# Attention score products in a two-layer kernel: row-mode steps planned as single products, sorted over the four row groups of TensorE

## The chip, the cores and the metric

The kernel runs on one core of a Trainium2 chip. The metric is the device time of one execution in microseconds (us). The kernel before takes 3334.01 us, the median of three runs (3331.4 to 3335.59). About 0.2% of this, some 7 us, is what a measurement of this kernel can tell from no change.

Engines are named as in the profile: PE is TensorE (PEld its weight loads), DVE is VectorE, ACT is ScalarE, POOL is GpSimd, SP is the queue that issues most DMAs.

## What is computed

The input x is (2, 2048, 256) in fp32. Each of two layers is `x = x + attn(norm(x)) * silu(ffn(norm(x)))`. The part that matters here is one causal softmax attention in each layer, with 16 heads of width 16 (first layer, inside its ffn) or 32 (second layer, where the real and the imaginary part of 16 each are one dot product of 32):

```python
scores = einsum('bhqd,bhkd->bhqk', q, k) / 4
scores = where(causal, scores, -1e9)          # -inf in the second layer
probs  = softmax(scores, axis=-1)
out    = einsum('bhqk,bhkd->bqhd', probs, v)
```

Around it the first layer has a linear attention, layer norms and a mixture of 8 experts (top 2, capacity 1024); the second has a quantized linear layer with a low-rank addition. All matrix products of scores and values are fp32.

## The kernel before

**Stages.** The first layer's attentions and routing run to about 1400 us, the experts to about 1917 us, the second layer's attention to the end.

**Heads and row groups.** Four heads form a group; a batch of 2 and 16 heads make 8 groups. A head's queries and keys lie in 32 partitions, so its score product needs 32 rows of the array, and the four heads of a group go to the four row groups 0 to 3 of PE, which work side by side ("row mode"; the profile shows such products as `32*128`). Sums of weighted values use four column groups ("col mode", `128*32`), and everything else the whole array ("all", `128*128`).

**Two passes over the scores.** Pass A (`pass_a`) computes scores of 128 queries by up to 512 keys, for the maximum of each query: L575 is the product (fp32, up to 512 columns), L594 the maximum on DVE over two heads at once. On the diagonal, the first layer adds the causal mask by four small bf16 products (`hide`, L534, 128, 96, 64 and 32 columns); the second layer masks on DVE instead (L588). Pass B (`pass_b`) computes the scores again, turned (keys by 256 queries): two products of up to 256 columns (L609), on the diagonal four bf16 mask products (`hide_pair`, L541, 256 down to 64 columns), in the second layer one or two bf16 products that subtract the maximum (`less_maximum`, L1697 to L1700), and then the exponential on ACT (L621). Sums over keys follow in col mode (L911, L1740, L1751); in the second layer POOL adds up the exponentials (L1717 to L1722).

**PSUM.** There are eight banks. A pair of heads of pass A takes two banks, one head of pass B takes one, and so does every other product. A bank comes free when DVE or ACT has read it.

**The order.** `run_attention` walks over units. A unit has one pass-A tile for the four heads of a group and, a little behind, one pass-B tile for four heads. Nothing is issued there: every piece of work becomes a step of a `Plan` (`S(strand, engine, cost, fn, reads, writes, on)`). Steps of one strand and engine stay in the order they were given. All row-mode and value-sum steps of PE form the strand "S"; other strands of PE (prep, lin, sub, end, mix, gate, ...) may go between them. `Plan.run` searches for an order: `advance` takes at each point the step that a model of the engines can start first (with offsets by strand), and a beam search varies the offsets. The steps are then issued in that order, engine by engine. So the order of all engines follows from the steps, their costs and the model.

**A unit's PE steps before.** For the heads i = 0, 1 of pass A and 2, 3 of pass B, and then the other way round: product A of head i, both products B of head i+2 as one step, product A of head i+1, both products B of head i+3 as one step; then the mask products, each head's four as one step (cost `T_HIDE_A` 0.15, `T_HIDE_B` 0.28).

**The model of PE before** (`advance`). A row group is taken until the cost of its last step has passed (`groups`); a step is handed out when its inputs are there and PE's queue is free, 0.01 us after the last; a load of 0.105 us is charged when a group was idle or the mode has just changed (`cold`).

Of the kernel before, what the change touches and what calls it, by code (L numbers as in the profile page):

```python
# [17 lines left out]
P = 128  # L18
# [76 lines left out]
class State:  # L95


    def __init__(self, plan):
# [9 lines left out]
        self.free, self.groups, self.cold = {}, [0.0] * 4, [True] * 4  # L108
# [12 lines left out]
class Plan:  # L121
# [101 lines left out]
    def advance(self, st, handicaps, until):  # L223

        free, groups, can, ready = st.free, st.groups, st.can, st.ready
        while st.todo:
# [4 lines left out]
            for key, s in can.items():  # L231
# [6 lines left out]
                if eng == "PE":  # L238
                    closed = strand != "S" and not (gap and st.used + s.cost <= self.LIMIT)
                    x = top if s.kind != st.mode else groups[s.on] if s.row else top - self.MODE  # L240
                    if x > busy:
                        busy = x
# [43 lines left out]
            if s.eng == "PE":  # L286
                st.used = st.used + s.cost if key[0] != "S" else 0.0
                kind = s.kind
                if kind != st.mode:
                    if kind == "row":  # L290
                        groups[:] = [max(t, x) for x in groups]
                    st.cold[:] = [True] * 4
                if s.row:
                    if t > groups[s.on] or st.cold[s.on]:
                        t += s.load
                    st.cold[s.on] = False
                elif t > max(groups) or st.cold[0]:
                    t += s.load
                    st.cold[0] = False
                done, free["PE"] = t + s.cost + self.TAIL - self.GAP, sent + 0.01  # L300
                if kind == "row":
                    st.mode, groups[s.on] = "row", t + s.cost
                    worth /= 4
                else:
                    st.mode, groups[:] = s.on, [t + s.cost] * 4
# [72 lines left out]
def kernel(ctx: ExitStack, tc: tile.TileContext, i: dict, out: bass.AP):  # L378
# [148 lines left out]
    T_HIDE_A, T_HIDE_B = 0.15, 0.28  # L527

    def hide(out, j, mask):

        r = slice(32 * j, 32 * j + 32)
        for q in range(4):
            cols = slice(32 * q, P)
            nc.tensor.matmul(out[:, cols], ident_h[r, q], mask[r, q, cols], start=False, stop=q == 3)  # L534

    def hide_pair(out, j, mask):

        r, v = slice(32 * j, 32 * j + 32), out.rearrange("p (n k) -> p n k", n=2)
        for q in (3, 2, 1, 0):
            cols = slice(0, 32 * q + 32)  # L540
            nc.tensor.matmul(v[:, :, cols], ident_h[r, q], mask[r, q, :, cols], start=False, stop=q == 0)  # L541
# [8 lines left out]
    def run_attention(plan, make, prepare, subtract, sum_keys, finish, last_sum, before=None, others=(), between=False, causal=None):  # L550
# [17 lines left out]
        def pass_a(g, t, k, i, w, mx, parts):  # L568
# [11 lines left out]
            def products(x):  # L580
                return S("S", "PE", t_row(w), lambda: score(x), r=[(g.qt, t), *((g.kt, n) for n in keys)], w=[(s, x)], on=i + x)

            def rest():
                for x in range(2) if diagonal and causal is None else ():
                    S("S", "PE", T_HIDE_A, lambda x=x: hide(s.t[:, x, w - P : w], i + x, mask_q), r=[(s, x), "ident_h", "mask_q"], w=[(s, x)], on=i + x)
# [15 lines left out]
        def pass_b(g, c, p, j, pt):  # L601
# [5 lines left out]
            def score():  # L607
                for n, (kj, q0, at) in enumerate(halves_of(c, p)):
                    nc.tensor.matmul(  # L609
                        s.t[:, at], g.kt.t[r, kj * P : (kj + 1) * P], g.qt.t[r, QC * c + q0 : QC * (c + 1)],  # L610
                        start=n == 0 and not ahead, stop=n == 1 and not (diagonal or before and not ahead),
                    )

            def rest():
                if before and not ahead:
                    S("S", "PE", 0.25 * t_row(w), before(g, c, j, s, diagonal, False, not diagonal), r=[s, g.mh[c]], w=[s], on=j, load=0.026)
                if diagonal:
                    S("S", "PE", T_HIDE_B, lambda: hide_pair(s.t[:, : 2 * P], j, mask_h), r=[s, "mask_h"], w=[s], on=j)
# [4 lines left out]
            reads = [(g.kt, 2 * p), (g.kt, 2 * p + 1), (g.qt, 2 * c), (g.qt, 2 * c + 1)]  # L623
            opener = None
            if ahead:
# [1256 lines left out]
```

## Time and profile before

| what | value |
|---|---|
| median of 3 runs | 3334.01 us |
| the profiled execution | 3333.86 us |
| its span, first to last instruction | 3332.1 us |
| mean granted TensorE clock | 0.982 |
| time up to the experts / the experts / second layer's attention | 0 to 1400 / 1400 to 1917 / 1917 to 3327 us |
| score products A (L575), records and busy time | 5120, 1282.3 us |
| score products B (L609), records and busy time | 9216, 1239.8 us |
| value sums (L911 and L1740) | 4608 records each, 269 us each |
| DVE maximum of two heads (L594), 1024 columns | 1221 ns |
| ACT exponential (L621), 512 columns | 602 ns |

How to read it: an fp32 product appears as two records, since it goes over the array twice (two "passes"); a bf16 product appears as one. A record of a matmul lasts from its start to the modelled end of its results, so the records of one group overlap, and the union "busy" says little about lost time. What tells the speed of a group is the distance between the starts of its records. In the timeline view, neighbouring records of one line are merged; a row gives start, length, engine, line, operation, tiles and shape, and a number of records.

### The profile page before, as it was taken

Reading aid. Unit: us, or ns where it says so; the run is one execution under the profiler, and the core shown is the slowest. Engines: PE = TensorE matmul, PEld = TensorE weight load, DVE = VectorE, ACT = ScalarE, POOL = GpSimd, SP = SyncE. Lnnn points to the kernel's source line nnn. Section 1 sums busy time; section 2 is a strip of 40 time slices with the busy share of each in tenths; the row PEclk is TensorE's granted clock in tenths of the full one; section 3 lists DMA queues with packets and bytes.
Section 4 is the critical chain, followed back from the end, with each engine's and each line's share of the span. In section 5 each row is a group of like instructions: output and inputs, shape, how many; then the busy total and the mean of one; then the engine's idle time right before and its main releaser. Section 6 shows DMA issues by size and latency. Waiting matters only on the chain.

```text
span 3332.1 us, 92022 instructions
## 1 busy us (share of the span) xinstructions
PE 3205.3 (96%) x39748; PEld 2271.7 (68%) x39748; DVE 2132.9 (64%) x4250; ACT 1623.4 (49%) x3264; POOL 1620.8 (49%) x2006
## 2 busy tenths in 40 slices
PE   7999999989999999979999989999999999999998
PEld 5677777767777776656666646666766666767775
DVE  5677677667777767641112057787777776777785
ACT  3565555555555555511112155555554555544554
POOL 5442222333233222310000057898987776878887
PEclk9999999999999999989999989999999999999999
DMA  5000000000000010133342131110101001000000
GB/s 198 2 2 2 5 8 8 17 30 26 6 11 5 9 45 13 49 109 115 109 131 94 64 105 43 38 43 29 39 17 33 27 17 40 23 12 23 14 29 24
DMA packets 99742, 134.51 MB, mean 40 GB/s; under 512 B 9461, under 2 KB 76739, under 8 KB 99334
## 3 DMA queue, kind: packets, MB, share of 16 engines
q1 hardware_dynamic: 93190, 114.74, 10.6%
q0 software_dynamic: 6144, 13.88, 1.3%
q8 instruction: 311, 5.10, 0.6%
q14 instruction: 97, 0.79, 0.1%
HBM read 93.75 MB, written 37.75 MB: 39 GB/s over the span
## 4 chain that ended last, share of the span: by engine, by line
PE 50%; DVE 3%; POOL 2%; ACT 1%; issue 1%; DMA 0%; POOLq 0%; another core or an unknown queue 0%; SPq 0%; DVEq 0%; ACTq 0%
PE banks L575 9%; PE banks L609 8%; PE banks L414 8%; PE banks L1740 7%; PE s L1488 7%; PE s L1494 7%; PE banks L1751 2%; PE banks L1700 1%; PE banks L541 1%; PE banks L1698 1%; DVE mx L594 1%; POOL ps L1721 1%; ACT pt L621 1%; POOL ps L1717 0%; POOL ps L1722 0%
## 5 line engine op out<-in xcount | busy, mean ns | idle before, releaser
L621 ACT ACTIVATE pt<-banks 128x512 f32<-128x512 f32 (+1 forms) x2304 | 1160.7, 577 | 721.9 <-PE banks L609 321.3
L594 DVE TENSOR_REDUCE mx<-banks 128x2 f32<-128x1024 f32 (+3 forms) x1024 | 1119.1, 1122 | 337.4 <-PE banks L609 141.7
L575 PE MATMUL banks<-carried,carried 32*128 32x512 f32 (+3 forms) x5120 | 1282.3, 566 | 25.0 <-DVE mx L594 10.5
L609 PE MATMUL banks<-carried,carried 32*128 32x256 f32 (+1 forms) x9216 | 1239.8, 378 | 3.8 <-issue 3.7
L609 PEld LDWEIGHTS banks<-carried,carried 32*128 32x128 f32 x9216 | 972.1, 186 | 42.8 <-issue 15.8
L575 PEld LDWEIGHTS banks<-carried,carried 32*128 32x128 f32 x5120 | 545.3, 185 | 242.3 <-issue 108.6
L1717 POOL TENSOR_TENSOR ps<-pt 128x1024 f32<-128x1024 f32 (+1 forms) x159 | 346.7, 2181 | 113.8 <-ACT pt L621 101.8
L1721 POOL TENSOR_TENSOR ps<-ps,pt 128x1024 f32<-128x1024 f32 x127 | 302.4, 2381 | 69.3 <-ACT pt L621 64.8
L848 POOL TENSOR_TENSOR ra<-raw,rope 128x128 f32<-128x128 f32 x128 | 60.1, 470 | 566.3 <-ACT raw L860 496.1
L1700 PE MATMUL banks<-mh,ones_h 3*128 3x512 bf16 x896 | 272.0, 382 | 7.5 <-ACT mh L1688 3.5
L1722 POOL TENSOR_TENSOR ps<-ps,pt 128x1024 f32<-128x1024 f32 (+1 forms) x127 | 269.1, 2119 | 10.0
L911 PE MATMUL banks<-pt,vt 128*32 128x256 f32 (+1 forms) x4608 | 269.1, 371 | 4.3 <-DVE mx L594 3.0
L1740 PE MATMUL banks<-pt,vt 128*32 128x256 f32 (+1 forms) x4608 | 269.0, 371 | 2.5 <-ACT pt L621 2.5
L1497 DVE TENSOR_TENSOR ye<-s,b 128x256 f32<-128x256 f32 x64 | 27.2, 424 | 380.6 <-PE s L1494 380.6
L588 DVE CUSTOM_DVE_ANT_0 banks<-banks,causal 128x384 f32<-128x384 f32 (+3 forms) x512 | 240.3, 515 | 40.5 <-PE banks L575 25.2
L1489 ACT ACTIVATE hm<-s,b1c 128x512 f32<-128x512 f32 x128 | 87.8, 687 | 347.2 <-PE s L1488 346.0
L1488 PE MATMUL s<-xt,carried 128*128 128x512 f32 x512 | 228.2, 604 | 9.7 <-DVE xt L1421 9.7
L1494 PE MATMUL s<-carried,hm 128*128 128x256 f32 x1024 | 223.6, 379 | 0.0
L1740 PEld LDWEIGHTS banks<-pt,vt 128*32 128x32 f32 x4608 | 135.2, 110 | 129.5 <-ACT pt L621 26.4
L1494 PEld LDWEIGHTS s<-carried,hm 128*128 128x128 f32 x1024 | 194.6, 190 | 33.3 <-issue 7.7
L911 PEld LDWEIGHTS banks<-pt,vt 128*32 128x32 f32 x4608 | 134.0, 109 | 114.4 <-issue 15.7
L1488 PEld LDWEIGHTS s<-xt,carried 128*128 128x128 f32 x512 | 97.4, 193 | 131.2 <-issue 110.2
(276 smaller groups left out, 4166.9 us busy)
## 6 DMA issues: line engine op xcount, KB each, us to landing
carried<-in_L_ffn_W_dram SPq DMA_DIRECT2D x32, 1024.0 KB
gl<-g_dram SPq DMA_DIRECT2D x64, 256.0 KB
slots_in<-zero SPq DMA_DIRECT2D x8, 1024.0 KB
slots_out<-ye SPq DMA_DIRECT2D x16, 512.0 KB
xe<-slots_in SPq DMA_DIRECT2D x15, 512.0 KB
s_dram<-lo SPq DMA_DIRECT2D x16, 256.0 KB
hn<-in_L_attn_x_dram SPq DMA_DIRECT2D x16, 256.0 KB
g_dram<-gs SPq DMA_DIRECT2D x16, 256.0 KB
```

Of the source, the lines that this page charges most:

```text
L575: nc.tensor.matmul(s.t[:, x, :w], g.qt.t[r, t * P : (t + 1) * P], g.kt.t[r, 512 * k : 512 * k + w], start=True, stop=not (diagonal and cau ...
L594: S("A", "DVE", t_dve(2 * w), lambda: nc.vector.tensor_reduce(mx.t[:, t % 2, i : i + 2, k], s.t[:, :, :w], AX.X, ALU.max), r=[(s, 0), (s, ...
L609: nc.tensor.matmul(s.t[:, at], g.kt.t[r, kj * P : (kj + 1) * P], g.qt.t[r, QC * c + q0 : QC * (c + 1)], start=n == 0 and not ahead, stop=n ...
L621: S("B", "ACT", t_act(w), lambda: nc.scalar.activation(pt.t[:, j, :w], s.t[:, :w], AF.Exp, scale=0.25), r=[s], w=[(pt, j)])
L911: nc.tensor.matmul(av.t[32 * j : 32 * j + 32, q0:QC], vts[G.vn][:, kj, j], pt.t[:, j, at], start=n == 0, stop=n == len(tiles) - 1,)
L1488: nc.tensor.matmul(ps, w1[:, k, f * P : (f + 1) * P], xt[:, k], start=k == 0, stop=k == 1)
L1494: nc.tensor.matmul(ps[:, :D], hm[:, f, s * P : (s + 1) * P], w2[:, f], start=f == 0, stop=f == FF // P - 1)
L1700: nc.tensor.matmul(s.t.rearrange("p (n q) -> p n q", n=2), ones_h[r], m[:, None].to_broadcast([3, 2, QC]), start=first, stop=last,)
L1717: nc.gpsimd.tensor_tensor(ps.t[:, :, q0:], pt.t[:, :, same], pt.t[:, :, odd], ALU.add)
L1721: nc.gpsimd.tensor_tensor(ps.t, ps.t, pt.t[:, :, even], ALU.add)
L1722: nc.gpsimd.tensor_tensor(ps.t[:, :, q0:], ps.t[:, :, q0:], pt.t[:, :, odd], ALU.add)
L1740: nc.tensor.matmul(av.t[32 * j : 32 * j + 32, q0:QC], G.vt.t[:, kj, j], pt.t[:, j, at], start=n == 0, stop=False)
```

## The change

1. `pass_a` and `pass_b` give their PE work as lists of single products: each mask product, each of the two products B, and each of the subtracting products is an entry of its own with its cost. The mask products of a head go in rising width instead of falling.
2. `run_attention` collects the entries of a whole unit in four queues, one for each row group (groups 0 and 1: A first, then B; groups 2 and 3: B first, then A). The summed costs of what is ahead give each entry the time at which the entry before it in its queue begins; entries are sorted by that time over all groups and become steps in this order. DVE and ACT steps follow after all PE steps of the unit. Steps of the paced strands (prep, lin, mix, gate) now wait for the unit's last PE step instead of its last product A.
3. The model: a row step cannot be handed out before the last step handed to its group has begun (`began`), so that a third step for one group holds PE's queue; a change of mode waits until all groups have ended, plus 0.1 us; the load is always counted from the time of handing out; a step takes 0.007 us of the queue instead of 0.01.

The arithmetic is the same. The core of the diff:

```diff
                 if eng == "PE":
+                    if s.row and s.kind == st.mode and began[s.on] > t:
+                        t = busy = began[s.on]
                     closed = strand != "S" and not (gap and st.used + s.cost <= self.LIMIT)
...
-                if kind != st.mode:
-                    if kind == "row":
-                        groups[:] = [max(t, x) for x in groups]
-                    st.cold[:] = [True] * 4
+                if s.kind != st.mode:
+                    sent = max(sent, max(groups) + self.MODE)
+                    st.mode, groups[:], began[:] = s.kind, [sent] * 4, [sent] * 4
                 if s.row:
-                    if t > groups[s.on] or st.cold[s.on]:
-                        t += s.load
-                    st.cold[s.on] = False
+                    t = max(groups[s.on], sent + s.load)
+                    began[s.on], groups[s.on] = t, t + s.cost
...
-                done, free["PE"] = t + s.cost + self.TAIL - self.GAP, sent + 0.01
+                done, free["PE"] = t + s.cost + self.TAIL - self.GAP, sent + 0.007
...
     def hide(out, j, mask):
-        for q in range(4):
-            cols = slice(32 * q, P)
-            nc.tensor.matmul(out[:, cols], ident_h[r, q], mask[r, q, cols], start=False, stop=q == 3)
+        for q in (3, 2, 1, 0):
+            cols = slice(32 * q, P)
+            parts.append((max(0.027, (P - 32 * q) / 2400), lambda q=q, cols=cols: nc.tensor.matmul(
+                out()[:, cols], ident_h[r, q], mask[r, q, cols], start=False, stop=q == 0
+            )))
...
             for i in (0, 2):
-                for x in range(2):
-                    if a:
-                        plan.pace = products(x)
-                        first = first or plan.pace
-                    if b:
-                        step, rest, weigh = pass_b(gb, cb, p, (i + 2 + x) % 4, pt)
-                        first = first or step
-                        more.append((rest, weigh))
-                if a:
-                    after_a()
-                for rest, _ in more:
-                    rest()
-                for _, weigh in more:
-                    weigh()
+                    for x in range(2):
+                        queues[i + x] += products(x)
+                    after.append(after_a)
+                for j in ((i + 2) % 4, (i + 3) % 4) if b else ():
+                    products, weigh = pass_b(gb, cb, p, j, pt)
+                    queues[j] += products()
+                    after.append(weigh)
+            order = []
+            for j, q in enumerate(queues):
+                began, until = -1.0, 0.0
+                for n, entry in enumerate(q):
+                    order.append((began, j, n, entry))
+                    began, until = until, until + entry[0]
+            order.sort(key=lambda x: x[:3])
+            for _, j, _, (cost, fn, r, w_, load) in order:
+                step = S("S", "PE", cost, fn, r=r, w=w_, on=j, load=load)
+                first = first or step
+            if a:
+                plan.pace = step
+            for call in after:
+                call()
```

## The prediction

> **What bounds the kernel now.** First the page: PE is busy nearly all the time in both attention stages, and the chain that ended last runs over PE where it can be followed.
>
> ```profile
> span 3332.1 us, 92022 instructions
> PE 3205.3 (96%) x39748; PEld 2271.7 (68%) x39748; DVE 2132.9 (64%) x4250; ACT 1623.4 (49%) x3264; POOL 1620.8 (49%) x2006
> ...
> PE 50%; DVE 3%; POOL 2%; ACT 1%; issue 1%; DMA 0%; POOLq 0%; another core or an unknown queue 0%; SPq 0%; DVEq 0%; ACTq 0%
> ```
>
> Then the windows of the three stages (length, busy time of PE, PEld, DVE, ACT, POOL):
>
> ```profile
> 10.00:1400.00 1390.00, 1350.05 (x17078) 998.39 (x17078) 986.48 (x1865) 779.37 (x1661) 448.05 (x1071) 0.99 0.07 23
> 1400.00:1917.00 517.00, 488.04 (x1840) 325.04 (x1839) 93.22 (x265) 106.59 (x160) 31.29 (x49) 0.97 0.32 105
> 1917.00:3327.00 1410.00, 1366.38 (x20833) 947.95 (x20831) 1050.28 (x2111) 734.27 (x1440) 1134.99 (x863) 0.98 0.11 33
> ```
>
> Only the first and third are touched. POOL fills 80% of the third, DVE 74%: they are next, not first. PE's "busy" is the union of four row groups, so one busy group hides three idle ones. The timeline of PE shows it, here in a run of row mode that began at 705.40 us:
>
> ```profile
> 705.94 0.61 PE L575 MATMUL banks<-carried,carried 32*128 32x512 f32 x2
> 706.16 0.39 PE L609 MATMUL banks<-carried,carried 32*128 32x256 f32 x2
> 706.37 0.23 PE L534 MATMUL banks<-mask_q,ident_h 32*128 32x128 bf16 x2
> 706.39 0.69 PE L575 MATMUL banks<-carried,carried 32*128 32x512 f32 x1
> 706.42 0.27 PE L534 MATMUL banks<-mask_q,ident_h 32*128 32x96 bf16 x6
> 706.52 0.46 PE L609 MATMUL banks<-carried,carried 32*128 32x256 f32 x1
> 706.53 0.69 PE L575 MATMUL banks<-carried,carried 32*128 32x512 f32 x1
> ...
> 707.72 0.42 PE L911 MATMUL banks<-pt,vt 128*32 128x256 f32 x4
> ```
>
> A pass of 512 columns takes 0.43 us (a product A starts its second pass at 705.94, its group goes on at 706.37), one of 256 half of that. The last passes of groups 2 and 3 start at 706.16 and 706.18, so the groups are free at 706.37 and 706.39. Their products A start at 706.39 and 706.53, both 0.69 long where a second pass is 0.59: their weights were not loaded ahead, which costs 0.105 more. Group 3 loses 0.14 + 0.105 with nothing to wait for. What stands ahead of it in the order are eight mask products and the products B of group 0. The starts fit one rule: **a group holds four passes** (an fp32 product is two, a bf16 product one), and a fifth holds all that stands behind it, for any group. The fourth mask of group 1 is such a fifth: it goes when A1 ends at 706.39, and only then does A2 load.
>
> **The sum, step by step.** I cut the order of PE at each change of mode. In the timeline the 339 row runs of the first layer take 702.8 us and the 253 of the second 766.8, together 1469.6.
>
> *Hold.* For each run I added up what its order alone costs: passes at 0.833 ns a column (fp32) or 0.417 (bf16, half of that row), four passes to a group, 0.0066 us between two hand-outs (the run's first four products start at 705.40, .41, .42, .43), a load of 0.105 after the pass before has begun (0.03 for bf16, the distance of the narrowest masks). This gives 608.0 + 655.5 = 1263.5 us. Against the timeline it leaves 0.07 us in the lower quartile and 0.08 in the median run of both layers: the drain before the next mode. At 0.075 over 592 runs that is 44 us; the other 162 us of the difference, in the upper half of the runs, are waits of PE for other engines. Without the limit of four the same sum is 568.7 + 587.3, so the hold is 39.3 + 68.2 = 107.5 us.
>
> The changed order, counted by the same rule, has 344 and 254 row runs of 572.9 + 584.3 = 1157.2 us, of which the hold is 0.6: entries now come in the order in which the groups can take them, masks no longer stand ahead of another group's scores. That the narrow mask comes first is in this sum (the load of what follows runs under the widest mask). Row runs: 1157.2 - 1263.5 = **-106**.
>
> *More changes of mode.* 1247 runs of one mode become 1279, 30 of them whole-array runs in the first layer (229 to 259). A change costs a drain of 0.075 and a load of up to 0.105: 32 x 0.18 = **+6**. From above: the mean whole-array run now loses 0.62 us to everything, 32 x 0.62 = +20.
>
> *What is given back to waits.* Where groups stall less, they come sooner to banks that DVE and ACT have not read. Two estimates.
> (a) From the trace of before: over the runs, I fitted the time above the longest group's passes to the hold of the run. In the first layer a microsecond of hold costs 1.1 us, in the second only 0.54: there, half of the stall covers a wait that comes anyway. Given back: 0 + 0.46 x 68 = 31.
> (b) From both orders: for each tile I took PE time from the end of the bank's last content to its new start, and set it against 1.221 us (DVE maximum) or 0.602 (ACT exponential) without any queue. Before, the reader has too little time in 120 of the runs, after in 267; the longest shortage of each run adds up to 34 and 89 us: +55.
> I take **+45**, between the two. The ends are 0 and 110 (the second rival's count).
>
> *What costs nothing.* The unit's DVE and ACT steps follow its PE steps in their own strands, on their own engines: their order among themselves stays. Paced steps wait for the unit's last PE step instead of the last product A, under 1 us later; PE has score work to cover it, and if that cover is gone it is a share of the 162 us. SP's list goes from 231 to 228 merged rows, the same DMAs in another sequence; the DMA share is 0.07 to 0.11 in these windows. POOL has 1135 us of work in the third stage; that stage would become some 1380 long, so POOL is next but does not close.
>
> Sum: -106 + 6 + 45 = -55. The profiled execution is 3333.86 (its span 3332.1, the median 3334.01): **3278 us**, 1.7% faster.
>
> Now a rule of the Trainium skill that speaks against this change. "TensorE: Matmul & The Clock Gate", section "Part 3: Packing small matmuls", says that PE has a reorder window of 64 and pulls a weight load ahead of matmuls in flight when it targets another row group. By it a full group would hold nobody, the hold would be 0 and the sum +6 us. The rows at 706.39 and 706.53 are against it: group 3's load came 0.14 us after its group was empty, and no load was pulled ahead.
>
> **Rivals.**
> 1. *The hold comes out whole.* For: the slope of 1.1 in the first layer; the new order was searched with a model that knows the hold, so it may place DVE's work better. Then -106 + 6: 3234.
> 2. *Slower: a wait at the head of PE's queue takes the place of the hold.* In the changed order the second product of each group is handed out near the start of a run, not after the masks. It carries its wait for a bank, and all groups stand behind it. Place: second layer, products A whose bank held a tile of pass A; DVE needs 1.22 us for two heads and PE gives it less. Counted to the hand-out instead of the start, the shortages go from 63 to 173 us, +110. The waits of before were 162 where this count says 63, so the count is no ceiling. It decides from 100 us more, 0.17 us on each of the 598 row runs. Against: waits of PE on DVE in before are short, as the next lines show (us, times, longest), and a wait in one run gives the next one time. At 1.1 times the count, -106 + 6 + 121: 3355.
>
> ```profile
> PE banks L575 <- DVE mx L594: 10.5, 22, 2.9
> PE banks L575 <- DVE mx L588: 2.9, 3, 1.9
> ```
>
> 3. *Most is given back* (80 to 95 us, estimate (b) times 1.5 to 1.7, with POOL and DVE fuller): 3318.
> 4. *It does not do what it says:* there is no such hold, the gaps at 706.39 and 706.53 are waits for banks; only the changes of mode stay: within 0.2%, 3338. Against: a quarter of the runs of both layers lie within 0.01 us of the rule and a constant drain.
>
> **How the numbers follow.** Forecast 3278 (say 3250 to 3308): 0.52. Rival 1 (below 3250): 0.22. Rival 3 (3308 to 3327): 0.09. Rival 4: 0.06. Rival 2: 0.11. Faster by over 0.2% (about what a measurement of this kernel can tell from no change): 0.52 + 0.22 + 0.09 = 0.83; same 0.06; slower 0.11. The range 3228 to 3332 leaves out the tip of rival 1 and nearly all of rival 2.
>
> **What would show it.** In the profile after: row runs without starts like 706.53 (a product 0.69 long in the middle of a run); row runs of some 1470 - 106 + 45 = 1410 us together; more idle PE and PEld time put down to DVE mx and ACT pt; DVE above 74% and POOL above 80% in the last stage; the experts' stage as long as before. I am wrong if the last stage gains more than the first (the fit says 37 against 39), or if the waits eat the whole.

## The result, and the profile after

The changed kernel takes 3505.26 us (median of four runs, 3503.68 to 3513.15); the kernel before, beside it on the same chip, 3334.8 (3331.4 to 3336.58). The ratio is 1.0517, with a 95% interval of 1.0499 to 1.0536: **5.2% slower, where 1.7% faster was forecast**. The profiled execution took 3503.68 us, 169.8 more than the one of before; the granted clock was 0.978 there and 0.982 before, so the clock can make 0.4% of the time at most, some 13 of these 170 us.

First the page of the changed kernel, in which product B is L610, the maximum L596 and the exponential L635 (span; busy time of the engines; then from the costliest groups: busy time and mean ns of one, and behind the second bar the idle time of the engine just before them, with what ended most of it):

```profile
span 3501.9 us, 92075 instructions
...
PE 3298.1 (94%) x39748; PEld 2126.3 (61%) x39748; DVE 2139.4 (61%) x4250; ACT 1627.5 (46%) x3266; POOL 1614.8 (46%) x2006
...
L635 ACT ACTIVATE pt<-banks 128x512 f32<-128x512 f32 (+1 forms) x2304 | 1160.6, 576 | 936.0 <-PE banks L610 497.7
L596 DVE TENSOR_REDUCE mx<-banks 128x2 f32<-128x1024 f32 (+3 forms) x1024 | 1123.6, 1121 | 412.0 <-PE banks L575 176.4
```

The same two groups in the page of before:

```profile
L621 ACT ACTIVATE pt<-banks 128x512 f32<-128x512 f32 (+1 forms) x2304 | 1160.7, 577 | 721.9 <-PE banks L609 321.3
L594 DVE TENSOR_REDUCE mx<-banks 128x2 f32<-128x1024 f32 (+3 forms) x1024 | 1119.1, 1122 | 337.4 <-PE banks L609 141.7
```

The work is the same: the exponential takes 576 ns as it did (577), the maximum 1121 (1122), and DVE, ACT and POOL are busy for as long as before, within 7 us. But ACT now stands idle 936.0 us ahead of its exponentials; before it was 721.9, with 321.3 put down to the products B. So PE gives the tiles of pass B later, and not because a reader (the instruction that reads a bank: DVE's maximum for pass A, ACT's exponential for pass B) got slower.

Next PE's own waits in the trace of the changed kernel (us, times, longest), those of its weight loads in the first fence, of its products in the second:

```profile
PEld banks L575 <- ACT pt L635: 71.8, 125, 2.2
...
PEld banks L575 <- DVE mx L596: 52.5, 95, 3.3
```

```profile
PE banks L575 <- ACT pt L635: 16.6, 30, 1.8
PE banks L575 <- DVE mx L596: 15.2, 34, 2.8
```

The same rows of before:

```profile
PEld banks L575 <- DVE mx L594: 49.8, 101, 3.4
...
PEld banks L575 <- ACT pt L621: 8.6, 17, 2.5
```

Waits of products A for a bank that the exponential still reads have gone from 8.6 to 71.8 us, and from 17 to 125 in number; those for DVE's maximum have hardly moved. These rows count only waits in which the engine is idle altogether, so they are a sign, not the sum.

For the sum I cut the order of PE at the changes of mode again, as in the prediction, and replayed each run with its semaphores: a product at the head of PE's queue whose bank is still being read holds all behind it until the reader's end in the trace. "Rule" is the time that the order alone costs with four passes to a group, "no hold" the same without that limit.

| us, both layers together | before | after | change | forecast |
|---|---|---|---|---|
| row runs in the trace | 1469.6 | 1609.8 | +140 | -61 |
| of it: no hold | 1156.0 | 1156.6 | +1 | |
| of it: hold (rule less no hold) | 107.5 | 0.6 | -107 | -106 |
| of it: all else | 206 | 453 | +246 | +45 |
| waits at the head of the queue, from the replay | 217 | 528 | +311 | |
| whole-array and col runs | 1848.2 | 1877.7 | +30 | +6 |

**The hold went as counted, and waits took its place more than twice over.** Of the 528 us of waits 291 are for ACT and 238 for DVE; before, 82 and 135. (These waits can add up to more than the row above them, since other groups still work under the first part of a wait.) The first layer's row runs lost 52 us and the second's 88. The row runs and the last row, +140 and +30, are the 169.8 us of the two profiled executions.

The timeline shows how a run now goes. First a run of the first layer in the changed kernel (start and length in us, engine, line, operation, tiles and shapes; the last figure of a row is the number of records; in brackets the idle time before it and what ended it):

```profile
617.71 0.70 PE L575 MATMUL banks<-carried,carried 32*128 32x512 f32 x2
...
617.73 0.70 PE L610 MATMUL banks<-carried,carried 32*128 32x256 f32 x4
...
618.14 0.59 ACT L1282 COPY lf<-banks 128x512 f32<-128x512 f32 x1 [1.56 <-issue]
...
618.26 0.79 PE L610 MATMUL banks<-carried,carried 32*128 32x256 f32 x6
...
618.69 0.78 PE L575 MATMUL banks<-carried,carried 32*128 32x512 f32 x2
...
618.89 0.60 PE L610 MATMUL banks<-carried,carried 32*128 32x256 f32 x4
...
619.12 0.78 PE L575 MATMUL banks<-carried,carried 32*128 32x512 f32 x2
...
619.40 1.57 ACT L635 ACTIVATE pt<-banks 128x512 f32<-128x512 f32 x3 [0.67 <-PE banks L610]
```

The groups alternate A and B as planned, and no group waits because another is full. The one product that starts late, product A of group 3 at 618.78 (the second of the row at 618.69), waited for its bank, which a copy on ACT read until 618.73. And the exponential starts at 619.40, and three follow one another: its first tile, that of group 2, had its last pass from 618.48 to 618.69 (618.85 with the modelled end). It waited 0.55 us more, because products B of groups 0 and 1 that stand ahead of that pass in PE's order ended at 619.27, and the signal to ACT came at 619.313. Those three tiles hold their banks all that time.

And a run of the second layer in the changed kernel, whose order costs 3.84 us by the rule and which took 6.17 (L1707 is the product that subtracts the maximum and opens a tile of pass B):

```profile
3268.21 0.39 PE L1707 MATMUL banks<-mh,ones_h 3*128 3x512 bf16 x2
3268.22 1.07 PE L575 MATMUL banks<-carried,carried 32*128 32x512 f32 x2
3268.93 0.86 PE L1707 MATMUL banks<-mh,ones_h 3*128 3x512 bf16 x2
3269.43 1.25 PE L610 MATMUL banks<-carried,carried 32*128 32x256 f32 x12
```

The tiles of groups 2 and 3 are opened at 3268.21, each taking a bank. The openers of groups 0 and 1 are handed out next, as second entries of their groups, and wait for exponentials on ACT; the products B of groups 2 and 3 stand behind them, until 3269.43. Two banks stand taken for 1.2 us, and but for the openers' own 0.2 us nothing is written to them.

I followed every bank through both orders, from the first write of a tile of pass B to the end of its last read (mean, us):

| tile of pass B | its own work on PE | open on PE | then to the end of its last read | total |
|---|---|---|---|---|
| first layer, before / after | 0.86 | 0.99 / 1.14 | 1.21 / 1.47 | 2.20 / 2.61 |
| second layer, before / after | 1.07 | 1.14 / 1.61 | 1.16 / 1.41 | 2.30 / 3.02 |

Tiles of pass A stay as they were (2.63 and 2.69 in the first layer, 2.42 and 2.45 in the second). So a bank of pass B is held 18% and 31% longer, and the next product that needs it comes to the head of the queue and finds it taken.

### The profile page after: what moved, and what is told of

It reads as the page before. It is cut to its first block, busy times and chain, and to the rows that moved or that the text cites. A ratio compares the mean times of both kernels' runs of the same rounds, so it can differ in the third digit from the quotient of the medians.

```text
span 3501.9 us, 92075 instructions
## 1 busy us (share of the span) xinstructions
PE 3298.1 (94%) x39748; PEld 2126.3 (61%) x39748; DVE 2139.4 (61%) x4250; ACT 1627.5 (46%) x3266; POOL 1614.8 (46%) x2006
## 5 line engine op out<-in xcount | busy, mean ns | idle before, releaser
L635 ACT ACTIVATE pt<-banks 128x512 f32<-128x512 f32 (+1 forms) x2304 | 1160.6, 576 | 936.0 <-PE banks L610 497.7
L596 DVE TENSOR_REDUCE mx<-banks 128x2 f32<-128x1024 f32 (+3 forms) x1024 | 1123.6, 1121 | 412.0 <-PE banks L575 176.4
L575 PE MATMUL banks<-carried,carried 32*128 32x512 f32 (+3 forms) x5120 | 1216.7, 567 | 51.2 <-ACT pt L635 16.6
L610 PE MATMUL banks<-carried,carried 32*128 32x256 f32 (+1 forms) x9216 | 1107.2, 388 | 6.0 <-DVE mx L590 2.8
L610 PEld LDWEIGHTS banks<-carried,carried 32*128 32x128 f32 x9216 | 756.6, 188 | 106.4 <-issue 39.2
L575 PEld LDWEIGHTS banks<-carried,carried 32*128 32x128 f32 x5120 | 445.4, 186 | 315.9 <-issue 120.0
L1707 PE MATMUL banks<-mh,ones_h 3*128 3x512 bf16 x896 | 198.1, 381 | 13.7 <-ACT pt L635 8.0
```

The lines of the kernel that those rows point to most:

```text
L575: nc.tensor.matmul(s.t[:, x, :w], g.qt.t[r, t * P : (t + 1) * P], g.kt.t[r, 512 * k : 512 * k + w], start=True, stop=not (diagonal and cau ...
L596: S("A", "DVE", t_dve(2 * w), lambda: nc.vector.tensor_reduce(mx.t[:, t % 2, i : i + 2, k], s.t[:, :, :w], AX.X, ALU.max), r=[(s, 0), (s, ...
L610: nc.tensor.matmul(s.t[:, at], g.kt.t[r, kj * P : (kj + 1) * P], g.qt.t[r, QC * c + q0 : QC * (c + 1)], start=n == 0 and not ahead, stop=n ...
L635: S("B", "ACT", t_act(w), lambda: nc.scalar.activation(pt.t[:, j, :w], s.t[:, :w], AF.Exp, scale=0.25), r=[s], w=[(pt, j)])
```

## Experiments

The edits are shown against the changed kernel, unless the text says against the kernel before. Ratios are to the kernel before on the same chip, with 95% intervals. That kernel took 3334.8 us on the chip of the result, 3336.25 on that of the runs by end and of the alternating masks and the whole heads by own start, and 3282 to 3285 on those of all others; so times in us of different chips are not compared. Where the replay needs a stand-in for before and after on the faster chips, the first two runs serve. In the expectations, 'order' and, later, 'early claim' name one theory: a product that is handed out early takes its bank early and blocks what stands behind it. Ranges in us were written with the chip of the result in mind.

**Model or steps?** The first two runs part the change in two: its steps with the model of before (the diff of `advance` turned back, its core below), and the steps of before with the new model (the same lines, put into the kernel before).

```diff
-                    if s.row and s.kind == st.mode and began[s.on] > t:
-                        t = busy = began[s.on]
...
-                    t = max(groups[s.on], sent + s.load)
-                    began[s.on], groups[s.on] = t, t + s.cost
+                    if t > groups[s.on] or st.cold[s.on]:
+                        t += s.load
+                    st.cold[s.on] = False
```

> The steps and their sorting as in the changed kernel, but the order is searched with the model of before. Theory 'order' (the sorting over a whole unit hands out the second entry of each group early, so banks are claimed early and held long, and PE's head of queue stalls on ACT and DVE): still slow, 3440 to 3560 us, product B tiles still hold a bank for 2.6 us in the first layer and 3.0 in the second. Theory 'model' (the search is led astray by a hold that is stricter than the chip's): back near before, 3300 to 3380 us.

> The steps and their sequence as before, but the order is searched with the new model (held by a group's third step, load always counted). Theory 'order': 3280 to 3350 us, B tiles hold a bank for 2.2 to 2.3 us as before. Theory 'model': 3440 to 3520 us. A third theory, 'split' (single products cost by themselves), expects 3280 to 3350 as well.

Measured: 1.0534 [1.0509, 1.0558] and 1.0025 [1.0016, 1.0035]. The new model alone costs a quarter of a per cent, and the changed steps cost the same with either model. In the steps of before with the new model the hold is still 106 us and the waits at the head of the queue 205, in the changed steps with the old model 0 and 509. **The whole loss is in the steps**, in what is handed out in which order; both runs came out as the theory of the order says.

**Claiming a bank early.** The sort gives each entry the time at which the entry *before* it begins. The next run gives it its own start, one entry later; the steps, the split and everything else stay:

```diff
-                began, until = -1.0, 0.0
+                until = 0.0
                 for n, entry in enumerate(q):
-                    order.append((began, j, n, entry))
-                    began, until = until, until + entry[0]
+                    order.append((until, j, n, entry))
+                    until += entry[0]
```

> As the changed kernel, but entries are sorted by the time at which they themselves begin, not the entry before them: each stands one entry later in the order. Theory 'order': 3330 to 3430 us, half or more of the 171 us comes back, and B tiles of the second layer hold a bank for under 2.7 us instead of 3.02. Theories 'model' and 'split': 3480 to 3530 us.

Measured: 1.0116 [1.0092, 1.0139]. **Nearly four fifths of the loss go with one change of the key** (5.17% to 1.16%), at a hold of 0. On the chip of the result that would be some 3374 us, in the range of the theory of the order, and a bank of pass B in the second layer is held 2.67 us, under the 2.7 that it named. First PE's weight loads on the exponential in this kernel, then ACT's idle time ahead of its exponentials:

```profile
PEld banks L575 <- ACT pt L635: 51.0, 103, 1.9
```

```profile
L635 ACT ACTIVATE pt<-banks 128x512 f32<-128x512 f32 (+1 forms) x2304 | 1166.5, 576 | 742.2 <-PE banks L610 361.5 <-PE banks L537 148.5 <-PE banks L575 107.6
```

ACT waits 742.2 us where it waited 936.0 in the changed kernel. It still gains nothing over before: beside the steps of before on an equally fast chip (the second run), the hold is 106 us less and the rest of the row time 118 more.

**Sorting within half a unit.** The steps of before never mixed the two halves of a unit. Here the queues and the sort are made for each half:

```diff
-            first, queues, after = None, [[] for _ in range(4)], []
+            first = None
             for i in (0, 2):
+                    queues, after = [[] for _ in range(4)], []
...
-            order = []
+                order = []
```

> As the changed kernel, but the entries are sorted within each half of a unit (heads 0 and 1 of pass A with 2 and 3 of pass B, then the other way round), so four banks are opened at a time as before the change. Theory 'order': 3270 to 3380 us. Theories 'model' and 'split': 3480 to 3530 us.

Measured: 1.0231 [1.0205, 1.0257]. The time in us lies in the range of the theory of the order, but only since this chip is 1.5% faster; by the ratio it missed that range, which asked for the loss to go. Half of it goes, the hold is 25 us, and in the second layer a tile stands open 1.46 us. With both edits, halves and own start:

> Sorted within halves of a unit and by the entries' own start: both remedies together. Theory 'early claim' (a bank is claimed when its first product is handed out, and the sorting hands it out early): 0.99 to 1.015 of the kernel before. If the remedies overlap fully: 1.01 to 1.02. If the loss were elsewhere: over 1.03.

Measured: 1.0196 [1.0177, 1.0215]; the two do not add up, as was expected if the remedies overlap fully. Once entries come at their own start, the halves only bring 32 us of hold back.

**How much hangs on the readers' length.** Both kernels with the maximum and the exponential over half the columns, so that banks come free sooner, the kernel before first (the maximum in the same way, and the rest of each output of the exponential set to 1.0 once):

```diff
-                S("B", "ACT", t_act(w), lambda: nc.scalar.activation(pt.t[:, j, :w], s.t[:, :w], AF.Exp, scale=0.25), r=[s], w=[(pt, j)])
+                S("B", "ACT", t_act(w), lambda: nc.scalar.activation(pt.t[:, j, : w // 2], s.t[:, : w // 2], AF.Exp, scale=0.25), r=[s], w=[(pt, j)])
```

> The kernel before, but the readers of the score banks do half of their work: the DVE maximum of pass A reads the first half of a tile's columns, the ACT exponential of pass B computes the first half (the rest of its output is 1.0, set once). The result is not the reference's; the order and all other work stay. Theory 'banks' (the row runs last as long as banks take to be read and come free; the hold lay on top of such waits): 0.96 to 0.985 of the kernel before, and not more, because the hold of 107 us stays. Rival 'PE' (hand-out and passes alone set the pace): 0.99 to 1.0.

> The changed kernel with the same halved readers (the same part of the computation left out). Theory 'banks': the loss goes, since banks come free sooner, and the hold that the change takes away now counts: 0.94 to 0.98 of the kernel before, level with the halved kernel before or faster. Rival 'PE' (the sorted order has a cost of its own in PE's queue, which no reader can take away): 1.03 to 1.05.

Measured: 0.9829 [0.9811, 0.9846] and 1.0107 [1.0087, 1.0127], a ratio of 1.0283 between the two, where it was 1.0517 with whole readers: between the two expectations. The exponential took 371 ns in place of 576. In the changed kernel with half readers:

```profile
L635 ACT ACTIVATE pt<-banks 128x256 f32<-128x256 f32 (+1 forms) x2304 | 717.4, 371 | 1066.3 <-PE banks L610 566.9
```

```profile
PEld banks L575 <- ACT pt L635: 43.7, 78, 1.9
```

**About half of the loss hangs on the length of the reading, half does not.** A bank that is claimed early, opened and left half filled, or released late, is taken longer whatever the reader takes; that this is the other half is argued, not shown. The waits in the replay fall in both kernels, to 107 and 370 us from 217 and 528 with whole readers; but their difference goes only from 311 to 263, so they do not follow the loss.

**A head of pass B as one entry.** All products of a head of pass B, openers too, as one entry, so that an opened tile is filled without a break:

```diff
+                def whole():
+                    for _, fn in openers:
+                        fn()
+                    for n, (kj, q0, at) in enumerate(halves):
+                        score(n, kj, q0, at)
```

> As the changed kernel, but all products of a pass-B head up to its masks are one entry, so nothing can stand between them; the whole-unit sorting by hand-out time stays. Theory 'early claim': still 1.035 to 1.055, since the second entry of a group is still handed out at the start of the unit. Theory 'interruption' (what costs is that an opened B tile stands half filled while PE's head waits for another tile's bank; 0.54 us a tile in the second layer): 1.00 to 1.025, and B tiles of the second layer open for under 1.25 us.

Measured: 1.0366 [1.0345, 1.0387], in the range of early claiming. Tiles of the second layer stand open 1.23 us in place of 1.61, yet only three tenths of the loss go; the hold is back at 114 us, since such an entry is four passes and more. The same entries sorted by their own start, with the edit of the key above:

> All products of a pass-B head are one entry and entries are sorted by their start: no bank wait inside an opened B tile, no early claim. Both theories of the loss ('early claim' and 'interruption') expect 0.995 to 1.010 of the kernel before and B tiles of the second layer open for under 1.25 us; some hold by five-pass entries comes back. If it stays over 1.015, something else costs.

Measured: 1.0343 [1.0319, 1.0367], where at most 1.01 was expected: **missed** by both theories. The hold is still 94 us and the waits 387; what costs the rest stays open.

**Later still.** Entries sorted by their end:

```diff
-                    order.append((began, j, n, entry))
-                    began, until = until, until + entry[0]
+                    until += entry[0]
+                    order.append((until, j, n, entry))
```

> As the changed kernel, but entries are sorted by the time at which they end. Theory 'signals in order' (PE tells its readers of finished work in the order of its program, so a tile that is done waits for every slower product handed out before it): signals of first-layer B tiles come under 0.08 us after their own end instead of 0.18, and the time is 0.998 to 1.010 of the kernel before, better than sorting by start (1.0116). Theory 'early claim' alone: as by start, 1.010 to 1.020.

Measured: 1.0616 [1.0584, 1.0647], the slowest of all and **missed**: the hold is back at 173 us, more than before, and the waits are 426. A likely reason, only argued, is that this key puts the short entries of one group ahead of the long ones of another, as the masks of before stood. The same with the second layer's opener joined to the first product B of its head (the diff stands further below, with the two runs that use it again):

> As sorting by end, and the second layer's subtracting product is one entry with the first product of its head, so its bank is claimed only when the product can follow. 'Interruption' and 'signals' together: 0.99 to 1.008 of the kernel before, and better than sorting by end alone in the second layer. If the opener does not matter: within 0.3% of sorting by end.

Measured: 1.0489 [1.0465, 1.0514]. That is outside both ranges. At about the same hold (179 us) it is 1.2% better than sorting by end alone; tiles of the second layer stand open 1.22 us.

**The hold alone.** The kernel before with its mask products split and those of the two heads of a half alternating, narrow ones first, so that no group gets four in a row:

```diff
-                for rest, _ in more:
-                    rest()
+                for calls in zip(*[rest() for rest, _ in more]):
+                    for call in calls:
+                        call()
```

> The kernel before with one part of the change alone: the mask products are single steps, in rising width, and alternate between the two heads of a half; the sequence of score products, the halves and the model stay as before. This takes most of the first layer's hold (39 us by the rule) away without opening a bank earlier. If the hold costs time: 0.985 to 0.994 of the kernel before. If PE would have waited anyway: 0.997 to 1.004.

Measured: 1.0086 [1.0068, 1.0104], outside both ranges. The rule gives 603.8 and 652.1 us of row time where it was 608.0 and 655.5, so the edit hardly touched the hold, and I had not seen that. The search found another order. Its stages (length, busy time of the five engines, then the granted clock):

```profile
10.00:1426.00 1416.00, 1374.91 (x17139) 995.79 (x17142) 982.58 (x1852) 784.88 (x1666) 450.50 (x1068) 0.97 0.07 23
1426.00:1946.00 520.00, 488.49 (x1784) 326.75 (x1773) 98.54 (x279) 104.21 (x154) 29.52 (x51) 0.96 0.32 104
1946.00:3360.00 1414.00, 1377.20 (x20817) 947.84 (x20815) 1051.17 (x2108) 736.68 (x1442) 1132.45 (x863) 0.98 0.10 32
```

The clock is lower than in the stages of before (0.99, 0.97, 0.98), and so it is in the timed runs: 0.975 in the mean of the six, where the eleven of the kernel before beside them had 0.980. Those eleven take 2.45 us more for each 0.001 of clock that they lack (a straight line through them), so by an estimate 12 of the 31 us go with the clock. The run tells nothing of the hold; what it tells is that **two kernels with nearly the same hold can lie half a per cent apart**, by the order that the search happens to find or by the split itself, which this run does not part. A difference of that size between two of these kernels proves little, and some 12 us of the loss of the run by end, which had a clock of 0.975 on the same chip, go with the clock by the same estimate.

**Early claim, or an opened tile that is interrupted?** After twelve runs it was open whether the early hand-out itself costs, or that an opened tile stands half filled as at 3268.21, or that the search's orders scatter. The joined opener with the key of the changed kernel, then with the own start; the edit of both is

```diff
-                if ahead:
-                    for cost, fn in before(g, c, j, s, diagonal, True, False):
-                        own.append((cost, fn, [g.mh[c]], [s], 0.026))
+                openers = before(g, c, j, s, diagonal, True, False) if ahead else []
...
+                    first_ = openers if n == 0 else []
...
+                    def fill(n=n, kj=kj, q0=q0, at=at, first_=first_):
+                        for _, fn in first_:
+                            fn()
+                        score(n, kj, q0, at)
```

> The changed kernel with the same joining alone; entries sorted by the start of the entry before, as in the changed kernel. Interruption: 1.03 to 1.043, tiles of pass B in the second layer open under 1.4 us (1.61 in the changed kernel). Early claiming alone: 1.047 to 1.055, since a group's second entry still comes out as early.

> The changed kernel with the second layer's subtracting products joined to the first product B of their head as one entry, and entries sorted by their own start. If a good part of the loss is that an opened tile of pass B stands half filled while other groups' entries wait for banks (interruption), this is better than sorting by own start alone (1.0116): 0.995 to 1.008, with tiles of pass B in the second layer open on PE for under 1.25 us in the mean (1.33 there). If only the early claim of banks counts, which is as in that run: within 0.3% of 1.0116.

Measured: 1.0533 [1.0511, 1.0555] and 1.0144 [1.0119, 1.0168], 0.28% above the run by own start alone: both in the ranges of early claiming. That **speaks against interruption as the main cause**, but does not rule it out: with the joining alone a tile of the second layer does stand open for less, yet 1.45 us, so only a third of what the change had added (1.14 to 1.61) is gone. Its signal to the reader comes 0.28 us after its own end (0.12 in the changed kernel), and it keeps its bank 3.04 us, no less than 3.02. So the 1.2% that the joining brought between the two runs sorted by end are not its doing in general.

And the key midway between the start of the entry before and the own start:

```diff
-                began, until = -1.0, 0.0
+                began, until = 0.0, 0.0
                 for n, entry in enumerate(q):
-                    order.append((began, j, n, entry))
+                    order.append((0.5 * (began + until), j, n, entry))
```

> The changed kernel with entries sorted by the middle between the start of the entry before and their own start. If the early claim is what costs, the loss follows the dose: 1.02 to 1.04, between the 1.0116 of the own start and the 1.0517 of the changed kernel. If the search's choice among orders makes the difference between those two, the middle need not lie between them.

Measured: 1.0194 [1.0173, 1.0215]. That lies between the two ends, as a dose should, though just below the range that was given and much nearer to the own start. Of the 4.0% between the two keys, moving entries half as far takes 3.2. On equally fast chips:

| steps, key | ratio | row runs | hold | waits at the head | bank of a pass-B tile, first / second layer |
|---|---|---|---|---|---|
| of before, new model | 1.0025 | 1442.9 | 106 | 205 | 2.12 / 2.23 |
| changed, own start | 1.0116 | 1454.7 | 0 | 465 | 2.31 / 2.67 |
| changed, midway | 1.0194 | 1474.2 | 0 | 505 | 2.30 / 2.74 |
| changed, start of the entry before, old model | 1.0534 | 1580.0 | 0 | 509 | 2.51 / 2.96 |
| the same with joined opener, new model | 1.0533 | 1594.7 | 18 | 550 | 2.50 / 3.04 |

With the changed steps, the earlier an entry is handed out, the slower the kernel, and in the second layer the longer a bank of pass B is held (in the first, own start and midway are alike). The waits at the head do not follow the ratio so well: the third and the fourth row have the same sum, and 106 us between their row runs. So the replayed sum of waits ranks the steps of before against the changed ones, but does not price the key.

No kernel here beats the one before; its steps with the new model come nearest.

## Why the prediction was wrong, step by step

**The hold: right.** Forecast -106 us by the rule of four passes, counted again in the order after: -107. The sign that the forecast named for it, no product of 0.69 us in the middle of a run, was badly chosen: the changed kernel still has such starts, as at 618.78, but from waits for a bank.

**More changes of mode: too small.** +6 taken, +20 as the upper end, +30 measured in whole-array and col runs together. Most of it, 17 us, lies in the whole-array runs of the first layer (436.2 to 453.2 us), which are 30 more: 0.57 us each, near the 0.62 of the upper end and three times the 0.18 that was taken. On the faster chips it is the same step, 426.1 us in the steps of before with the new model and 443.8 with the joined opener. So a further run cost more here than a drain and a load.

**"What is given back to waits": this step failed.** +45 was taken, with ends of 0 and 110; everything in the row runs beside the rule rose by 246. Neither estimate could have seen it.
- Estimate (a) asked how much of a stall covers a wait, by comparing runs *of the old order*, and the fit was loose: done again over all row runs of that trace its slopes come out at 0.85 and 1.26 in place of 1.1 and 0.54, each with a standard error of 0.25, and at 0.86 and 0.21 when the length of the run is let in as well. It could not tell a stall that is given back from one that is not. And the new order does not only take the hold out, it hands the second product of each group out one entry early. The runs by key show that this is what costs: at the same hold of 0 and the same entries the ratio goes from 1.0116 over 1.0194 to 1.0517.
- Estimate (b) counted the PE time that each reader has between a bank's last content and its new start, and took a bank as free 0.602 us after its own last product. In the trace exponentials come close together (three in a row at 619.40) and are released late, and the tile itself is open longer than its products need (1.61 us for 1.07). A tile of pass B keeps its bank 0.4 to 0.7 us longer than before with an exponential of the same length.
- Even by own start, 118 us came back for 106 of hold. So the stall of before was no time to be had in any order tried here. That the banks came free in it is the likely reason, but no run takes the hold out and leaves the banks as they were. I had priced that at 0.46 in one layer and at 0 in the other.

**What costs nothing: right.** DVE and POOL did not become the bound, as the window of the last stage in the changed kernel shows (from 2050 us on; length, busy time of PE, PEld, DVE, ACT, POOL): DVE fills 71% and POOL 76% of it. The experts' stage is about as long as before: its whole-array run takes 510.1 us (506.6 before), begins 73 us later and ends 77 us later; the end of the kernel is 170 us later, so the last stage has 93.

```profile
2050.00:3500.00 1450.00, 1386.63 (x20262) 840.51 (x20259) 1030.61 (x2035) 710.14 (x1390) 1107.86 (x831) 0.98 0.09 27
```

I had named DVE above 74% and POOL above 80% as signs of the forecast, so both speak against it. PE's "busy" is 1386.63 of 1450, 96% where it was 97%: the union of four groups hides the whole loss, as it hid the hold.

**Rival 2 was the one that came, at a chance of 0.11.** Its mechanism is right: a wait at the head of PE's queue in place of the hold, since a group's second product is handed out near the start of a run. Its price, 121 us, was half of the 246, and its place was too narrow: it looked for products A of the second layer behind DVE, while of the 311 us that the waits rose, 209 are waits for ACT, and both layers lost. I held against it that PE's waits on DVE are short in the page of before (10.5 us in 22). Those rows count only times when all of PE is idle; the replay of the same trace has 217 us of waits at the head, in 537 places. What I noted beside the rival, that the count is "no ceiling", was the sentence to follow.

**What stays open.** How the 246 us part among the earlier claim, the tiles that stand open and the late signals: no edit moved one without the others (the joining shortens the standing open and makes the signal later). That about half hangs on the readers' length is shown (1.0283 with half readers); why the rest does not is argued from the three, not shown. A kernel in which each signal comes with its own group was not tried. Nor is it parted what the 1.2% by own start are made of: the new model (a quarter of a per cent by itself), the later pacing, the split into single steps, the search's order and banks that are still held longer than before (2.67 us for 2.23 in the second layer) are all in it.

## What to carry to other kernels

An order that keeps four row groups full is not yet a fast one: in a queue that hands out in order, each entry also claims its bank and blocks all behind it, so hand out a product no earlier than its group can start it (the key by own start; by end, with the hold back, was slower again), and count how long each bank is held from first write to last read before and after. A stall that the profile shows may be the time in which another resource comes free; what removing it brings is bounded by an experiment (here: shorter readers, a later key), not by a fit over runs that all contain it. And where a search sets the order, a difference of half a per cent may be the search's own, or the clock's.

## What the runs showed of the hardware

**Four passes to a group.** The rule on which the prediction rests can be tried with other limits on the trace of before. Over the 546 row runs of six products or more, 35% end within 0.01 us of the rule and one constant with a limit of four. With three, runs end up to 0.8 us sooner than the rule allows; with five, or none, some 20% fit, and the median run ends 0.2 us later against the rule than with four.

**Signals leave PE in the order of its program, across row groups.** A product's semaphore goes up only when every product ahead of it has ended: in the changed kernel the updates come at a median of 0.014 us after the last end of all products up to then. In the run at 617.71 a tile of group 2 that was ready at 618.69 (618.85 with the modelled end) was signalled at 619.313, since products B of groups 0 and 1 ahead of it ended at 619.27. The mean delay for tiles of pass B was 0.02 us in both layers before, and 0.18 and 0.12 after; with the joined opener 0.28 in the second layer. The Trainium skill, "TensorE: Matmul & The Clock Gate", section "Part 3: Packing small matmuls", says that matmuls start and end in program order, so that one semaphore increment on the last is enough. The increments agree with it here; the records do not, across row groups: in that run second products of groups 2 and 3 start at 618.26, ahead of products of groups 0 and 1 that stand before them in the program and start at 618.68.

**The same program on other chips.** The kernel before took 3334.8 us beside the changed kernel and 3336.25 on the chip of four later runs, and 3281.76 to 3284.65 on three others, 1.5% apart, at mean granted clocks of about 0.98 and 0.985. In the first layer, the same order of row runs took 755.0 us in the changed kernel and 732.7 in the one with joined openers, on chips of either kind. The joined openers are of the second layer alone, and the order of the first layer is the same, so this is not the edit. The trace has the clock at one half for 37.5 us of that stage in the slower execution and for 6.8 in the faster; 31 of the 38 us by which the stages differ lie in the runs that this touches, and the median run is as long in both.
